# A routed feed-forward kernel: starting-up products ahead of the styles, a shorter list for the first expert, and its tokens turned and multiplied group by group

## The chip, the cores and the metric

The kernel runs on one core of one Trainium2 chip. The metric is the device time of one execution in microseconds (us). Five engines work side by side and are joined by semaphores: TensorE (PE; its weight loads are listed apart as PEld), VectorE (DVE), ScalarE (ACT), GpSimd (POOL) and SyncE (SP). SP and POOL also issue DMA transfers.

## What is computed

With B = 8 samples of L = 512 rows and C = D = 512 channels (N = 4096 rows), E = 8 experts of width 2048, and K = 1024 rows per expert:

```
styles = cond @ (affine_w / 16).T + affine_b          # 8 x 512
dcoefs = rsqrt(sum((weight * styles)**2) + 1e-8)      # 8 x 512
y      = clip(((x * styles) @ weight.T) * dcoefs + bias, -256, 256)
scores = softmax(y @ Wr)                              # 4096 x 8
G, idx = top_k(scores.T, 1024)                        # each expert takes its 1024 best rows
h      = gelu(y[idx] @ W1 + b1)                       # per expert, 1024 x 2048
out    = x + scatter_add(idx, G * (h @ W2 + b2))
```

Everything is float32. `idx` is a data-dependent list, so an expert's rows are fetched from memory with indirect DMAs, and they can't be fetched before the list is known.

## The kernel before

**Stage 1, the projection (0 to about 139 us).** The styles are the first work on TensorE: two products of `cond_sb` with `aff_sb` (lines 389 to 392; a float32 product is two instructions, so four), then one DVE operation (`style_rows`, line 395) and a turn back to columns (`turn_style`, line 403). Sample 0 is turned with TensorE (`turn_x0`, line 375), scaled and multiplied; samples 1 to 7 follow in `unit` (line 569). `in_order` (line 366) chains TensorE instructions so that they are issued in the order written; where it isn't used, the framework puts an engine's instructions into an order of its own, subject to data dependences. For each sample `score_softmax` (line 515) makes the eight scores of each row (`S`), the first expert's score (`S0`), copies of it (`reps`) and, against 64 thresholds, a table `ge` that is summed into `topc`.

**Stage 2, the first expert's list (139 to 162 us).** `route_first` (line 205) adds up the eight `topc` tables on TensorE (`tot_top`), picks the leading six bits of the threshold, finds the other 24 bits in six rounds of four (line 220: one DVE count, one TensorE product, three small DVE steps), marks the rows and ranks them; `lo` and `hi` are the rank's low seven bits and the rest. Meanwhile TensorE turns five late samples and SP stores them in `y_dram` (lines 698 to 708). `indices` (line 810) makes one-hot tables of `lo` (`oh`, 128 wide, in four parts for expert 0) and `hi` (`hot`, 8 wide), and multiplies them for the 32 groups of 128 rows (line 835, 32 products), which gives the 8 x 128 row numbers `idx`.

**Stage 3, the first expert's tokens (162 to about 182 us).** `fetch(0)` (line 1098) issues eight indirect DMAs on POOL (`gather`, line 865), groups 0 to 3 (the first half, i = 0) and then 4 to 7 (i = 1), each of 128 rows; after them POOL issues the copy of x to the output (line 1112). `prepare(0)` (line 890) turns each group with four TensorE instructions (line 910), copies the result to `xT` with two DVE copies (line 912), and at the end makes four sums of the halves (`left_sums`, line 881), each over 128 x 1024 elements, on DVE.

**Stage 4, the experts (from then to the end).** For each expert two passes of `hidden_unit` (line 956; four units `u`, each with 128 hidden columns of either half of the pass) and `out_unit` (line 1011). Both use a scheme of seven block products in place of eight: p1 = "11", p2 = "12", p6 = "s2", p7 = "s3", p5 = "s1", p3 = "s4", p4 = "22", where s1 to s4 are the sums. A product is four TensorE instructions of 128x512 in a hidden unit and eight of 128x256 in an output unit, all issued in `product` (line 950), so they stand under line 953 in the profile (`ps_a_h`, `ps_b_h`, `ps_c_h` for the hidden units). `in_turns` (line 924) runs the units, each one's last two products behind the first ones of the next; `between` puts other work behind a unit, such as `route_others` (line 713), which finds the other seven experts' lists on DVE behind unit 0 of the first pass. Buffers: the PSUM banks `a` and `c` exist twice, `b` once, `ps_t` (for turning) twice; the SBUF tag `xg` twice (the gathered tokens, and before them the one-hot table).

Of the kernel before, what the change touches and what calls it, by code (L numbers as in the profile page):

```python
# [25 lines left out]
def tile_modulated_expert_choice_ffn(  # L26
# [26 lines left out]
    GH = HALF // P  # L53
    GAIN = 1.0 / math.sqrt(W)
# [18 lines left out]

    ident = const.tile([P, P], F32, name="ident")
# [3 lines left out]
    ones = const.tile([P, P], BF16, name="ones")  # L78
    nc.gpsimd.memset(ones, 1.0)
# [22 lines left out]
    iota_hi = const.tile([P, KG], BF16, name="iota_hi")  # L102
    nc.gpsimd.iota(iota_hi, pattern=[[1, KG]], base=0, channel_multiplier=0,
# [15 lines left out]
    NR = (30 - TOP) // RB  # L119
    M = 1 << RB  # L120
# [84 lines left out]
    def route_first(p1c, reps, topc):  # L205
# [6 lines left out]
        for n in range(B):  # L212
            nc.tensor.matmul(tot, ones, topc[:, n, :], start=(n == 0), stop=(n == B - 1))
# [6 lines left out]
        for n in range(NR):  # L220
# [24 lines left out]
        nc.tensor.matmul(ps[:, 0, :, :].rearrange("p a t -> p (a t)"), ones, flat,  # L245
                         start=True, stop=True)
        nc.tensor.matmul(ps[:, 1, :, :].rearrange("p a t -> p (a t)"), upper, flat,
                         start=True, stop=True)
# [23 lines left out]
        nc.vector.tensor_scalar(part, pos_i, P - 1, None, op0=ALU.bitwise_and)  # L272
# [3 lines left out]
        nc.vector.tensor_scalar(part2, pos_i, 7, None, op0=ALU.logical_shift_right)  # L276
# [13 lines left out]
    with tc.tile_pool(name="p1c", bufs=1) as p1c, tc.tile_pool(name="p1", bufs=2) as p1, \  # L290
# [72 lines left out]

        behind = {}

        def in_order(make, engine="PE"):

            if engine in behind:
                with tc.issue_after(behind[engine].ins):
                    behind[engine] = make()  # L370
            else:
                behind[engine] = make()
            return behind[engine]
# [141 lines left out]
        def score_softmax(b, ps):  # L515

            lgT = p1s.tile([P, P], F32, tag="lgT", name=f"lgT_{b}", bufs=2)
            nc.scalar.copy(lgT, ps)
            lg4 = ps_small.tile([P, LT, SL], F32, tag="small", name=f"lg_{b}")
            in_order(partial(nc.tensor.transpose, lg4.rearrange("p t e -> p (t e)"), lgT, ident))  # L520
            lg = lg4[:, :, 0:E]
            mx = p1s.tile([P, LT], F32, tag="mx", name=f"mx_{b}")
            nc.vector.tensor_reduce(mx, lg, AX.X, ALU.max)
            ex = p1s.tile([P, LT, E], F32, tag="ex", name=f"ex_{b}")
            nc.vector.tensor_tensor(ex, lg, mx.unsqueeze(2).to_broadcast([P, LT, E]), ALU.subtract)
            nc.scalar.activation(ex, ex, AF.Exp)
            sm = p1s.tile([P, LT], F32, tag="sm", name=f"sm_{b}")
            nc.vector.tensor_reduce(sm, ex, AX.X, ALU.add)
            nc.vector.reciprocal(sm, sm)
            here = slice(b * LT, (b + 1) * LT)  # L530
            nc.vector.tensor_tensor(S[:, here, :], ex,
                                    sm.unsqueeze(2).to_broadcast([P, LT, E]), ALU.mult)
            nc.vector.tensor_copy(S0[:, here], S[:, here, 0])
            nc.vector.tensor_copy(reps[:, :, :, b],
                                  S0[:, here].unsqueeze(2).to_broadcast([P, ST_G, M]))
            ge = p1s.tile([P, 1 << TOP, LT], BF16, tag="getop", name=f"getop_{b}", bufs=2)
            nc.vector.tensor_tensor(ge, S0[:, here].unsqueeze(1).to_broadcast([P, 1 << TOP, LT]),
                                    top.bitcast(F32).unsqueeze(2).to_broadcast([P, 1 << TOP, LT]),
                                    ALU.is_ge)
            with nc.allow_low_precision("whole numbers up to 4"):  # L540
                nc.vector.tensor_reduce(topc[:, b, :], ge, AX.X, ALU.add)
# [150 lines left out]
        score_softmax(B - 1, lg)  # L692
# [3 lines left out]
        places = {0: route_first(p1c, reps, topc)}  # L696
# [113 lines left out]
    def indices(e):  # L810
# [7 lines left out]
            iota_hi.unsqueeze(1).to_broadcast([P, NT, KG]), ALU.is_equal,  # L818
# [6 lines left out]

        parts = 1 if e else 4
        for n in range(parts):
            here = slice(n * NT // parts, (n + 1) * NT // parts)
            nc.vector.tensor_tensor(  # L829
                oh[:, here, :], lo[:, here].unsqueeze(2).to_broadcast([P, NT // parts, P]),  # L830
                iota_lo.unsqueeze(1).to_broadcast([P, NT // parts, P]), ALU.is_equal,
            )
# [7 lines left out]
        nc.vector.tensor_copy(idx[:, e, :], idx_f)  # L840

# [10 lines left out]
    def gather(e, i):  # L852

        z = gp.tile([P, GH * YW], F32, tag="xg", name=f"xg_{e}_{i}")
        if e:
            rows = dram.tile([HALF, YW], F32, name=f"rows_{e}_{i}")
            z = z[:, 0 : GH * D].rearrange("p (t c) -> p t c", c=P)
        else:  # L860
            z = z.rearrange("p (g w) -> p g w", w=YW)
        for j in range(GH):
            g = i * GH + j
            to = gp.tile([P, YW], F32, tag="row", name=f"row_{e}_{g}", bufs=4) if e else z[:, j, :]
            sent = nc.gpsimd.indirect_dma_start(
                out=to[:, :], out_offset=None, in_=y_dram[:, :],
                in_offset=bass.IndirectOffsetOnAxis(ap=idx[:, e, g : g + 1], axis=0),
            )
            if e:
                nc.sync.dma_start(rows[j * P : (j + 1) * P, :], to)  # L870
        if e:
            for q in range(4):
                nc.sync.dma_start(z[q * TB : (q + 1) * TB, :, :],
                                  rows[:, q * P : (q + 1) * P].rearrange("(t a) c -> a t c", a=TB))
            with nc.allow_non_contiguous_dma(reason="512 values"):
                nc.sync.dma_start(gains[e][:, i * GH : (i + 1) * GH],
                                  rows[:, D + e : D + e + 1].rearrange("(g p) o -> p (g o)", p=P))
        gathered[e, i] = z
        return sent
# [9 lines left out]

    def prepare(e):  # L890

        xT = {}
        for i in range(2):
            for k in range(2):
                xT[i, k] = fx.tile([P, 2, HALF], F32, tag=f"xT{i}{k}", name=f"xT{i}{k}_{e}")
        gain = gains.pop(e)
        ngain = fx.tile([P, KG], F32, tag="ngain", name=f"ngain_{e}")
        for i in range(2):
            xg = gathered.pop((e, i))
            for k in range(2):  # L900
                if e:
                    nc.vector.transpose(
                        xT[i, k].rearrange("p j (t b) -> p t j b", b=TB),
                        xg[:, :, 2 * k * TB : 2 * (k + 1) * TB].rearrange("p t (j a) -> p t j a", a=TB))
            for j in range(0 if e else GH):
                g = i * GH + j
                nc.scalar.copy(gain[:, g : g + 1], xg[:, j, D + e : D + e + 1])
                ps = ps_t.tile([P, DC, P], F32, tag="t", name=f"ps_xg{e}_{g}")
                for dc in range(DC):
                    nc.tensor.transpose(ps[:, dc, :], xg[:, j, dc * P : (dc + 1) * P], ident)  # L910
                for k in range(2):
                    nc.vector.tensor_copy(xT[i, k][:, :, j * P : (j + 1) * P],
                                          ps[:, 2 * k : 2 * k + 2, :])
        nc.vector.tensor_scalar_mul(ngain, gain, -1.0)
        s = {n: fx.tile([P, 2, HALF], F32, tag=f"x{n}", name=f"x{n}_{e}")
             for n in ("s1", "s2", "s3", "s4")}
        left_sums(xT[0, 0], xT[0, 1], xT[1, 0], xT[1, 1], s)
        s["11"], s["12"], s["22"] = xT[0, 0], xT[0, 1], xT[1, 1]
        tokens[e] = s, gain, ngain
# [35 lines left out]

    def hidden_unit(e, p, u, H):

        s, _, _ = tokens[e]
# [6 lines left out]
        def mm(ps, left, right, start):  # L965
            product(ps, [blk[right][:, k, u * P : (u + 1) * P] for k in range(2)],
                    [s[left][:, k, :] for k in range(2)], start)

# [5 lines left out]
        def p1():  # L974
            st["a"] = bank("a", name, 2)
            mm(st["a"], "11", (0, 0), True)
            st["s1"] = snap(1)

        def p2():
            st["b"] = bank("b", name, 1)  # L980
            mm(st["b"], "12", (1, 0), True)
# [27 lines left out]
        return [p1, p2, p6, p7, p5, p3, p4]  # L1009
# [88 lines left out]
    def fetch(e):  # L1098
# [3 lines left out]
        for i in range(2):  # L1102
            sent = gather(e, i)
        return sent
# [5 lines left out]

    with tc.issue_after(fetch(0).ins):
        nc.gpsimd.dma_start(out.rearrange("b l d -> b (l d)").rearrange("b (r w) -> (b r) w", r=16),
                            x.rearrange("b l d -> b (l d)").rearrange("b (r w) -> (b r) w", r=16))
    prepare(0)
    for e in range(E):
        b2_sb = fx.tile([P, D], F32, tag="b2", name=f"b2_{e}")
        nc.sync.dma_start(b2_sb, b2[e, :].partition_broadcast(P))
        for p in range(NP):
            nxt = (e, p + 1) if p + 1 < NP else (e + 1, 0)
            H = fx.tile([P, U, 2, KG * P], F32, tag="H", name=f"H_{e}_{p}")  # L1120
# [5 lines left out]
            in_turns([partial(hidden_unit, e, p, u, H) for u in range(U)], work)  # L1126
# [48 lines left out]
```

## Time and profile before

| what | value |
|---|---|
| time, median of 3 runs | 1750.04 us (1749.76 to 1750.58) |
| the profiled execution's own time | 1749.67 us |
| its span, first to last instruction | 1747.9 us |
| PE busy in the span | 1708.3 us (98%) |
| DVE / ACT / POOL busy | 835.7 / 478.3 / 292.2 us |
| PE busy from 0 to 30 us | 23.86 of 30 us |
| PE busy from 152 to 172 us | 6.15 of 20 us |
| PE busy from 262 us to the end | 1474.83 of 1485.9 us |

The profiled execution took 1.8 us more than its span and 0.37 us less than the median. "Busy" counts an instruction from its start to its modelled end; TensorE instructions overlap, so what one of a row costs is read from the distance between starts. "PEclk" is the share of the full TensorE clock that was granted. The release of a wait is inferred; "issue" means that nothing the profile shows was waited for.

### The profile page before, as it was taken

The numbers are of one execution on the slowest core, as the hardware profiler recorded it, in microseconds if no ns is written. First come the engines' busy times: TensorE is split into PE (matmuls) and PEld (weight loads), VectorE is DVE, ScalarE is ACT, GpSimd is POOL, SyncE is SP. The second block draws the span as 40 slices with busy tenths as digits, with TensorE's granted clock in tenths as the row PEclk, the third lists the DMA queues.
The fourth block names the chain that finished last, engine by engine and source line by source line (L and its number), as shares of the span: only waits on it lengthen the run. The fifth ranks groups of instructions, "written<-read, shape, count | busy, mean of one in ns | idle before, by whom it ended". The sixth has DMA issues, their size and how long they took to land.

```text
span 1747.9 us, 17152 instructions
## 1 busy us (share of the span) xinstructions
PE 1708.3 (98%) x6522; PEld 1128.9 (65%) x6522; DVE 835.7 (48%) x1465; ACT 478.3 (27%) x842; POOL 292.2 (17%) x238
## 2 busy tenths in 40 slices
PE   8995999999999999999999999999999999999997
PEld 4774475665748485666748485766758484756656
DVE  5885883624536254524535254614445254614341
ACT  3543312223131322223231313222231313222231
POOL 0112013020222013020312013110312012110202
PEclk9997999999999999999999999999999999999999
DMA  9625627541573227441574237442574137332403
GB/s 205 172 50 177 211 49 165 121 90 48 96 201 67 54 52 173 109 84 50 98 197 79 48 64 179 89 80 55 108 184 88 45 66 182 79 79 61 84 0 49
DMA packets 143250, 178.57 MB, mean 102 GB/s; under 512 B 16824, under 2 KB 92856, under 8 KB 143040
## 3 DMA queue, kind: packets, MB, share of 16 engines
q1 hardware_dynamic: 118240, 115.19, 24.5%
q0 software_dynamic: 24912, 62.27, 21.1%
q8 instruction: 51, 0.84, 0.2%
q14 instruction: 31, 0.25, 0.1%
q10 hardware_dynamic: 16, 0.02, 0.0%
HBM read 120.46 MB, written 65.37 MB: 106 GB/s over the span
## 4 chain that ended last, share of the span: by engine, by line
PE 87%; DVE 2%; issue 0%; DMA 0%; POOLq 0%; POOL 0%; DVEq 0%
PE ps_a_o L953 25%; PE ps_a_h L953 25%; PE ps_c_o L953 12%; PE ps_c_h L953 12%; PE ps_b_h L953 6%; PE ps_b_o L953 6%; DVE mark L736 0%; PE ps_idx L835 0%; DVE oh L829 0%; DMA xg<-y_dram,idx 0%; PE ps_xg L910 0%; DVE ps_b_h L982 0%; POOLq L1171 0%; DVE hs_o L884 0%; DVE hs_o L883 0%
## 5 line engine op out<-in xcount | busy, mean ns | idle before, releaser
L1065 POOL DMA_INDIRECT out<-o_o,idx x128 | 212.3, 1659 | 1248.8 <-DVE o_o L1062 553.2
L953 PE MATMUL ps_a_o<-w_t,hs_o 128*128 128x256 f32 x1024 | 243.6, 380 | 1.2
L953 PE MATMUL ps_a_h<-xs,w_t 128*128 128x512 f32 x512 | 241.1, 593 | 0.0
L953 PEld LDWEIGHTS ps_a_o<-w_t,hs_o 128*128 128x128 f32 x1024 | 192.3, 190 | 33.4 <-issue 7.0
L971 ACT COPY snap_h<-ps_a_h 128x512 f32<-128x512 f32 x192 | 111.7, 582 | 236.9 <-PE ps_a_h L953 231.8
L953 PEld LDWEIGHTS ps_a_h<-xs,w_t 128*128 128x128 f32 x512 | 97.0, 190 | 123.0 <-issue 122.1
L1032 ACT ACTIVATE snap_o<-ps_a_o,gain 128x256 f32<-128x256 f32 x128 | 60.6, 474 | 347.5 <-PE ps_a_o L953 347.5
L997 DVE TENSOR_TENSOR snap_h<-snap_h,ps_c_h 128x512 f32<-128x512 f32 x64 | 43.9, 686 | 217.5 <-ACT snap_h L971 217.5
L982 DVE TENSOR_TENSOR ps_b_h<-ps_b_h,snap_h 128x512 f32<-128x512 f32 x64 | 44.7, 699 | 202.9 <-PE ps_b_h L953 202.9
L953 PE MATMUL ps_a_h<-xT,w 128*128 128x512 f32 x256 | 125.6, 598 | 0.0
L953 PE MATMUL ps_a_o<-w,H 128*128 128x256 f32 x512 | 124.1, 379 | 0.0
L953 PE MATMUL ps_c_o<-w,hs_o 128*128 128x256 f32 x512 | 123.8, 379 | 0.0
L953 PE MATMUL ps_a_h<-xs,w 128*128 128x512 f32 x256 | 122.0, 599 | 0.0
L953 PE MATMUL ps_a_o<-w,hs_o 128*128 128x256 f32 x512 | 121.5, 380 | 0.0
L953 PE MATMUL ps_b_o<-w,H 128*128 128x256 f32 x512 | 121.2, 379 | 0.0
L953 PE MATMUL ps_b_h<-xT,w 128*128 128x512 f32 x256 | 120.8, 593 | 0.0
L953 PE MATMUL ps_c_h<-xs,w 128*128 128x512 f32 x256 | 120.5, 593 | 0.0
L953 PE MATMUL ps_c_h<-xT,w_t 128*128 128x512 f32 x256 | 120.5, 593 | 0.0
L953 PE MATMUL ps_c_o<-w_t,H 128*128 128x256 f32 x504 | 119.1, 379 | 0.0
L953 PEld LDWEIGHTS ps_a_o<-w,H 128*128 128x128 f32 x512 | 97.1, 190 | 27.0 <-issue 15.5
L953 PEld LDWEIGHTS ps_a_o<-w,hs_o 128*128 128x128 f32 x512 | 96.0, 190 | 21.4 <-ACT snap_o L1032 8.9
L953 PEld LDWEIGHTS ps_c_o<-w,hs_o 128*128 128x128 f32 x512 | 97.1, 190 | 14.0 <-issue 0.6
(248 smaller groups left out, 1935.9 us busy)
## 6 DMA issues: line engine op xcount, KB each, us to landing
w<-in_w SPq DMA_DIRECT2D x120, 512.0 KB, 4.0
rows<-row SPq DMA_DIRECT2D x56, 260.0 KB, 4.0
xg<-rows SPq DMA_DIRECT2D x56, 256.0 KB, 6.6
x<-in_x SPq DMA_DIRECT2D x28, 256.0 KB, 8.8
y_dram<-ytok SPq DMA_DIRECT2D x5, 1024.0 KB, 4.4
w<-in_w SPq DMA_DIRECT2D x32, 128.0 KB, 4.1
y_dram<-ytok POOLq DMA_DIRECT2D x12, 256.0 KB, 4.8
b<-in_b SPq DMA_DIRECT2D x8, 256.0 KB, 4.0
```

Of the source, the lines that this page charges most:

```text
L953: nc.tensor.matmul(ps, lefts[k], rights[k], start=(start and k == 0), stop=(k == n - 1), skip_group_check=True)
L971: nc.scalar.copy(t, st["a"])
L982: added = nc.vector.tensor_add(st["b"], st["b"], st["s1"])
L997: nc.vector.tensor_add(st["u4"], st["u4"], st["c"])
L1032: nc.scalar.mul(t, st["a"], scale)
L1065: nc.gpsimd.indirect_dma_start(out=last_rows[g] if e == E - 1 else out_rows, out_offset=bass.IndirectOffsetOnAxis(ap=idx[:, e, g : g + 1], ...
```

## The change

- A helper `idle` issues products of a constant table of ones with itself (128x512 in bf16) into an unused bank; nine are issued ahead of the first product of the styles. The table `ones` is filled ahead of the other constants. `in_order` and its chain now serve the whole kernel.
- In `score_softmax`, `S0` is made straight from the exponentials and their sums. For the last sample `S` is made after `ge`, and `ge` isn't summed on DVE: `route_first` adds its four columns per threshold with four products.
- The first expert's rank is split into six low bits (`LO` = 64) and the rest (`HI` = 16): `first_indices` takes the place of `indices(0)`. The one-hot table of the low digits is half as wide, that of the high ones twice, one of the two products of the latter goes to ACT, and each of the 32 groups takes two TensorE products of 64 weight columns each, into partitions 0 to 63 and 64 to 127. Each part's products are issued behind the part.
- `first_tokens` takes the place of `gather(0, i)` and `prepare(0)`: groups are fetched in the order 0, 4, 1, 5, 2, 6, 3, 7. For each pair both groups are turned, the first half is copied by DVE and the second by ACT, the four sums are made for these 128 columns, and p1 and p2 of hidden units 0 and 1 are made for these 128 columns (`begin`). The gains are copied in two instructions at the end.
- `gather` and `prepare` lose their branches for expert 0.

```diff
+    IDLE0 = 9
+    def idle(n, ps):
+
+        for _ in range(n):
+            in_order(partial(nc.tensor.matmul, ps.rearrange("p (a k) -> p a k", k=P), ones,
+                             ones.unsqueeze(1).to_broadcast([P, HALF // P, P]), start=True, stop=True))
+
+    ones = const.tile([P, P], BF16, name="ones")
+    nc.gpsimd.memset(ones, 1.0)
+    idle(IDLE0, ps_mm.tile([P, HALF], F32, tag="c", name="ps_idle0", bufs=2))
...
+    LO, HI = P // 2, 2 * KG
...
-        for n in range(B):
-            nc.tensor.matmul(tot, ones, topc[:, n, :], start=(n == 0), stop=(n == B - 1))
+        for n in range(B - 1):
+            nc.tensor.matmul(tot, ones, topc[:, n, :], start=(n == 0), stop=False)
+        for t in range(LT):
+            nc.tensor.matmul(tot, ones, last_top[:, :, t], start=False, stop=(t == LT - 1))
...
-            nc.vector.tensor_copy(S0[:, here], S[:, here, 0])
+            last = b == B - 1
+            if not last:
+                scores()
+            nc.vector.tensor_mul(S0[:, here], ex[:, :, 0], sm)
...
+            if last:
+                with tc.issue_after(done.ins):
+                    scores()
+                return ge
...
+    def first_indices():
+
+
+        lo, hi = places[0]
+        hot = gp.tile([P, 2 * GH * YW], BF16, tag="xg", name="hot_0")[:, 0 : NT * HI].rearrange(
+            "p (t h) -> p t h", h=HI)
+        nc.vector.tensor_tensor(hot, hi.unsqueeze(2).to_broadcast([P, NT, HI]),
+                                iota_hi.unsqueeze(1).to_broadcast([P, NT, HI]), ALU.is_equal)
...
+        nc.scalar.mul(val[:, :, 0, :], hot, iota_p[:, 0:1])
+        nc.vector.tensor_tensor(val[:, :, 1, :], hot,
+                                iota_t.unsqueeze(2).to_broadcast([P, NT, HI]), ALU.mult)
+        parts = 4
+        ps = ps_small.tile([P, 2, KG], F32, tag="small", name="ps_idx0")
+        for n in range(parts):
+            here = slice(n * NT // parts, (n + 1) * NT // parts)
+            nc.vector.tensor_tensor(
+                oh[:, here, :], lo[:, here].unsqueeze(2).to_broadcast([P, NT // parts, LO]),
+                iota_lo[:, 0:LO].unsqueeze(1).to_broadcast([P, NT // parts, LO]), ALU.is_equal)
+            for t in range(NT)[here]:
+                for q in range(P // LO):
+                    in_order(partial(
+                        nc.tensor.matmul, ps[q * LO : (q + 1) * LO, :, :], oh[:, t, :],
+                        val[:, t, :, :].rearrange("p a (g q) -> p q a g", q=P // LO)[:, q, :, :],
+                        start=(t == 0), stop=(t == NT - 1), skip_group_check=True))
...
+    def first_tokens(started):
+
+
+        half = [gp.tile([P, GH * YW], F32, tag="xg", name=f"xg_0_{i}").rearrange(
+            "p (g w) -> p g w", w=YW) for i in range(2)]
+        for j in range(GH):
+            for i in range(2):
+                g = i * GH + j
+                sent = nc.gpsimd.indirect_dma_start(
+                    out=half[i][:, j, :], out_offset=None, in_=y_dram[:, :],
+                    in_offset=bass.IndirectOffsetOnAxis(ap=idx[:, 0, g : g + 1], axis=0))
...
+        xT, s, gain, ngain = token_tiles(0)
+        for j in range(GH):
+            cols = slice(j * P, (j + 1) * P)
+            for i in range(2):
+                ps = ps_t.tile([P, DC, P], F32, tag="t", name=f"ps_xg_{i}_{j}")
+                for dc in range(DC):
+                    in_order(partial(nc.tensor.transpose, ps[:, dc, :],
+                                     half[i][:, j, dc * P : (dc + 1) * P], ident))
+                for k in range(2):
+                    if i:
+                        copied = nc.scalar.copy(xT[i, k][:, :, cols], ps[:, 2 * k : 2 * k + 2, :])
+                    else:
+                        nc.vector.tensor_copy(xT[i, k][:, :, cols], ps[:, 2 * k : 2 * k + 2, :])
+            left_sums(*[xT[i, k][:, :, cols] for i in range(2) for k in range(2)],
+                      {n: t[:, :, cols] for n, t in s.items()})
+            for f in started:
+                f(cols)
...
+        def begin(cols):
+            s = tokens[e][0]
+
+            for to, left, right in (("a", "11", (0, 0)), ("b", "12", (1, 0))):
+                if to not in st:
+                    st[to] = bank("c" if u and to == "b" else to, f"{name}_{to}", 1 if to == "b" and not u else 2)
+                for k in range(2):
+                    in_order(partial(nc.tensor.matmul, st[to][:, cols],
+                                     blk[right][:, k, u * P : (u + 1) * P], s[left][:, k, cols],
+                                     start=(cols.start == k == 0), stop=(k == 1),
+                                     skip_group_check=True))
...
-    with tc.issue_after(fetch(0).ins):
-        nc.gpsimd.dma_start(out.rearrange("b l d -> b (l d)").rearrange("b (r w) -> (b r) w", r=16),
-                            x.rearrange("b l d -> b (l d)").rearrange("b (r w) -> (b r) w", r=16))
-    prepare(0)
+    first_indices()
+    gains[0] = fx.tile([P, KG], F32, tag="gain", name="gain_0", bufs=2)
+    H = fx.tile([P, U, 2, KG * P], F32, tag="H", name="H_0_0")
+    early = [hidden_unit(0, 0, u, H, early=True) for u in range(2)]
+    first_tokens([begin for begin, _ in early])
```

## The prediction

> **What bounds the kernel now.** I read the page's 40 slices first, then the busy time and clock by stretches, then the instructions in order of time in three places that the change touches. From 262 us on TensorE is busy for 1474.83 of 1485.9 us, and nothing of that part is changed; so I ask only how much earlier TensorE gets there. Two places are loose: the first 30 us and 152 to 172 us.
>
> ```profile
> PE   8995999999999999999999999999999999999997
> ...
> 148.00:152.00 4.00, 2.17 (x14) 1.47 (x14) 2.85 (x13) 1.79 (x4) 0.00 (x0) 1.00 1.01 376
> 152.00:156.00 4.00, 0.22 (x2) 0.10 (x1) 3.28 (x19) 0.00 (x0) 0.00 (x0) 0.76 0.50 190
> 156.00:160.00 4.00, 0.77 (x17) 0.59 (x17) 4.00 (x6) 0.00 (x0) 0.00 (x0) 0.50 0.21 70
> 172.00:176.00 4.00, 3.85 (x16) 2.55 (x16) 2.21 (x7) 0.76 (x4) 1.56 (x2) 0.68 1.28 437
> 176.00:178.00 2.00, 2.00 (x9) 1.15 (x8) 1.76 (x7) 1.38 (x3) 0.00 (x0) 1.00 0.82 328
> ```
>
> In the stretches the columns are PE, PEld, DVE, ACT, POOL, then the granted clock, the DMA share and GB/s. The fourth slice (131 to 175 us) is the 5; in it the clock falls to half at about 154 and is back in about 174.7.
>
> ```profile
> 4.98 1.87 PE L372 MATMUL ps_style<-aff_sb,cond_sb 128*8 128x512 f32 x2 [4.98 <-DMA cond_sb<-in_condT]
> 6.64 1.91 PE L370 MATMUL ps_style<-aff_sb,cond_sb 128*8 128x512 f32 x2
> 8.48 1.98 PE L370 MATMUL ps_x<-ident,x 128*128 128x128 f32 x8
> 8.59 1.08 DVE L395 SCALAR_TENSOR_TENSOR style_rows<-ps_style,affb_in 8x512 f32<-8x512 f32 x1 [2.98 <-PE ps_style L370]
> 10.40 0.64 PE L370 MATMUL ps_styleT<-ident,style_rows 8*128 8x8 f32 x4
> 12.75 3.60 PE L370 MATMUL ps_y<-xmT,wa_sb 128*128 128x512 f32 x8
> ```
>
> The clock column says 1.00 here, but the distances say otherwise: four style instructions take 3.5 us (0.87 each), the same size at 12.75 takes 0.45. TensorE starts slow and is fast from some point after 10.4.
>
> ```profile
> 138.59 0.42 DVE L537 TENSOR_TENSOR getop<-S,top 128x256 bf16<-128x256 f32 x1
> 139.04 0.42 DVE L541 TENSOR_REDUCE topc<-getop 128x64 bf16<-128x256 bf16 x1
> 139.81 0.23 DVE L216 SCALAR_TENSOR_TENSOR ok_top<-tot_top,top 128x64 f32<-128x64 f32 x1 [0.35 <-PE tot_top L213]
> ...
> 156.45 4.62 DVE L829 TENSOR_TENSOR oh<-lo,iota_lo 128x1024 bf16<-128x1024 bf16 x4
> 161.13 0.38 PE L835 MATMUL ps_idx<-val,oh 128*128 128x16 bf16 x8 [0.75 <-DVE oh L829]
> 163.16 1.04 POOL L865 DMA_INDIRECT xg<-y_dram,idx  x1 [23.88 <-issue]
> ...
> 166.65 1.12 PE L910 MATMUL ps_xg<-ident,xg 128*128 128x128 f32 x4 [5.14 <-DMA xg<-y_dram,idx]
> 173.03 1.80 PE L953 MATMUL ps_a_h<-xT,w 128*128 128x512 f32 x2
> 176.84 1.88 PE L953 MATMUL ps_b_h<-xT,w 128*128 128x512 f32 x4
> ```
>
> From 133 to 162 a chain of small DVE steps ends last; from 162 to 176 the eight fetches, which POOL issues about 1.27 us apart; from 176.7 on TensorE.
>
> [...]work from 4.98 is slow past 10.4, work from 168.1 is slow until 174.7[...]. [...]No row of before has 64 bf16 columns. [...]the trace has 0.42 us for 256 elements and 1.22 for 1024[...], also for these bf16 tables.
>
> **1. Nine products ahead of the styles.** `ones` is filled in 0.2 us from 0.75, so they can start at about 1.05. A bf16 one of 512 columns should take half a slow float32 instruction of 0.87 (estimate 0.43), nine 3.85 us: they end at 4.9, where `aff_sb` lands (4.95), so they delay the styles by nothing, at worst by one product. [...]the clock rises between about 4.2 and 7.6. Averaged, the four style instructions end at 7.2 instead of 8.42. The DVE row step follows 0.17 later and takes 1.08, so the styles can be turned at 8.55. Before they waited until 10.39, because the eight slow turns of x ended then; fast turns of 0.11 end at about 8.1. That is 1.84, and the turn of the styles itself falls from 0.64 to about 0.41: **2.0 us** (1.1 to 2.5). The weights `wa_sb` land 6.2 to 6.7 after issues at 2.8 to 4.2, at 9.0 to 10.9, so products at 10.7 find them, and x_1 lands by about 21 and is wanted at 22.9. From 30 to 130 TensorE is busy for 97.3 us, waits for DMAs nowhere, so the gain is handed on whole.
>
> **2. The last sample's scores.** S0 comes one DVE step earlier (138.05 instead of 138.27: 0.22). The sum of `ge` (139.04 to 139.46) goes; four products take the place of one (some 0.03 apart by the six at 129.99: 0.1), and may queue behind the four turns of `reps` (0.66). Of 0.6 I count **0.35** (0.1 to 0.6). Making S after `ge` lies in DVE's wait for TensorE, and its store has 20 us. The seven earlier samples change a copy for a product: nothing.
>
> **3. The list.** DVE: `hot` and the second product grow from 256 to 512 elements, +0.27 each; the first product goes to ACT, -0.20 (155.91 to 156.11); the first part of `oh` has 512 elements, not 1024, -0.53. So TensorE starts at 157.5 instead of 157.72. ACT is idle there; its product takes about 0.6 and is done by 157.0. The parts then come 0.60 apart[...]. TensorE has 16 pairs a part: the 128 columns of before came 27 ns apart (0.38 for eight, less a last one of 0.19) at the half clock. [...]TensorE is the bound, and its 64 pairs end at 161.0 instead of 161.5: **0.5 us**. At 27 ns DVE would be the bound and the gain 1.6; at 67 (load and product in turn) it is -0.4. The bank and number of fetches are as before, and so is the 1.23 us from `idx` to the first.
>
> **4. The tokens.** Fetches are as many and as far apart; I use the old landing times, 166.5 to 175.7. A pair takes eight turns and 16 pieces of 128 columns (2 units x 2 products x 2 k x 2 instructions). Slow, at 0.213 each, that is 5.1 us; fast, with 0.114 for a turn (the late samples: eight in 0.91) and 0.107 for a piece (a quarter of 0.43; two weight loads in 0.30 show that loads can follow at 0.11), 2.6, plus about 0.3 for the first DVE copy (0.2 + 0.38 after the turns of the first half, with the second's turns beside them). Pairs land 2.5 apart, so TensorE, not the fetch, is now the bound: pair 0 from 166.65 to 172.4, clock up at about 173 (171.5 to 174.9), pairs 1 to 3 end at 175.6, 178.5 and 181.3. DVE has 0.76 + four sums of 256 elements (1.5) a pair, 2.3, which lies beside it; the last sums are there at 181.6. ACT's two copies (0.85) and later the table load (1.28) have cover too: p6 and p7 take 3.4 us of TensorE before p5 wants ACT's second copy. By 181.6 the new kernel has 16 instructions of line 953 done. Before it had 14 at 181.35 (2+2+4+2+4), so 14.6, and had made the turn of S (0.22). So 1.4 x 0.43 - 0.22: **0.4 us** (-0.2 for a late clock, 1.1 for an early one).
>
> The sum is 2.0 + 0.35 + 0.5 + 0.4 = 3.25 us. Against 1749.67 of the profiled execution that gives **1746.4 us**. That execution is 0.37 under the median of 1750.04; I leave that[...]. Where the moved start of `route_others` falls changes nothing that I can price: TensorE waited only 1.1 us for it.
>
> **Rivals.**
> - *The list and the tokens give more*: 64 columns load in 27 ns (+1.1), and TensorE is woken by the idle-free run of 64 pairs[...] (+0.7 to 1.1). 1749.67 - 5.2 = 1744.4. For it: weight loads of 32 float32 columns stand 25 ns apart. Against it: the five idle us of the fetch lie between.
> - *The start is not handed on*: [...]the styles wait behind the ninth product; part 1 gives 0.7 and the tokens nothing: 1748.3.[...] Against it: no wait for a DMA stands behind the styles.
> - *Slower: pieces bound by weight loads.* If the load of a piece can't lie beside the piece before, as long as itself, each costs 0.107 + 0.19 (the mean load) = 0.30. 64 x 0.19 = 12 us more: 1758.6. It turns the sign from 0.16 a piece on. Against it: turns have as short a product and come 0.114 apart, with a load each.
>
> **Chances.** Forecast 0.53, more 0.24, start not handed on 0.17, slower 0.06. About 0.2% (3.5 us, 1746.54) can be told from no change. The forecast lies on that line and half of it counts as faster, 0.29, half as the same, 0.24; "more" is faster, "not handed on" the same, the last slower. Faster 0.53, same 0.41, slower 0.06. The range takes in "more" to its far end and "not handed on": 1743.6 to 1748.9; what is left out is the slow rival and the far tails.
>
> **What would show it.** Nine products from about 1 to 4.9, and ps_styleT near 8.6 instead of 10.40; the first fetch at about 160.3 (163.16 less 2.85); products of `ps_idx` 53 ns apart, ending after DVE; pieces 0.11 apart; TensorE without gaps from about 165 to 178, shifted. It is wrong if the styles are turned at 10, if the pieces come 0.2 or more apart, or if TensorE waits for sums after the last pair by more than 1 us.

## The result and the profile after

The changed kernel takes **1746.51 us** (median of 17 runs, 1744.58 to 1748.62) where the one before, beside it, takes 1749.87 (1748.92 to 1753.08, 17 runs): ratio 0.9981, 95% interval [0.9974, 0.9988]. The 17 runs lie in two groups: eight from 1744.58 to 1746.08 (middle 1745.69), eight from 1747.08 to 1748.62 (middle 1747.69), one between. The profiled execution is of the later group: 1747.71 us, span 1745.9. It is 1.96 under the profiled one of before (1749.67).

The page's slices first, TensorE's share and its clock, in tenths:

```profile
PE   9996999999999999999999999999999999999997
...
PEclk9998999999999999999999999999999999999999
```

Where before had an 8 in the first slice and a 5 in the fourth there is now a 9 and a 6. The stretches (PE, PEld, DVE, ACT, POOL, granted clock, DMA share, GB/s) put the difference at the list:

```profile
148.00:152.00 4.00, 2.06 (x16) 1.43 (x14) 2.73 (x14) 2.18 (x4) 0.00 (x0) 1.00 0.99 360
152.00:156.00 4.00, 0.22 (x2) 0.10 (x1) 3.03 (x16) 0.00 (x0) 0.00 (x0) 0.76 0.58 214
156.00:160.00 4.00, 2.35 (x64) 2.05 (x64) 3.30 (x7) 0.72 (x1) 0.00 (x0) 0.50 0.29 70
...
172.00:176.00 4.00, 3.84 (x32) 3.51 (x32) 3.19 (x10) 1.29 (x4) 0.10 (x1) 1.00 1.09 391
176.00:178.00 2.00, 2.00 (x20) 1.86 (x18) 1.36 (x4) 0.00 (x0) 0.00 (x0) 1.00 1.05 426
```

The start, in order of time (start, duration, engine, line, operation, count, and in brackets the idle time ahead and who ended it):

```profile
1.41 3.13 PE L81 MATMUL ps_idle<-ones 128*128 128x512 bf16 x8
...
5.05 1.88 PE L81 MATMUL ps_style<-aff_sb,cond_sb 128*8 128x512 f32 x4 [0.51 <-DMA cond_sb<-in_condT]
...
6.96 1.05 DVE L405 SCALAR_TENSOR_TENSOR style_rows<-ps_style,affb_in 8x512 f32<-8x512 f32 x1 [1.36 <-PE ps_style L81]
7.96 0.99 PE L81 MATMUL ps_x<-ident,x 128*128 128x128 f32 x6 [0.60 <-DMA x<-in_x]
8.88 0.64 PE L81 MATMUL ps_styleT<-ident,style_rows 8*128 8x8 f32 x4
...
10.68 1.10 PE L81 MATMUL ps_x<-ident,x 128*128 128x128 f32 x4 [1.16 <-DVE xmT L81]
11.58 4.88 PE L81 MATMUL ps_y<-xmT,wa_sb 128*128 128x512 f32 x8
16.30 0.63 PE L81 MATMUL ps_x<-ident,x 128*128 128x128 f32 x4
```

The styles are turned at 8.88, not 10.40: 1.52 gained. But the eight products of `ps_y` that follow take 4.88 us where before they took 3.60, and the next turns of x stand at 16.30 against 16.19 before. Against this profile of before, the start gained nothing.

The scores, the list and the first tokens:

```profile
138.33 0.42 DVE L553 TENSOR_TENSOR getop<-S,top 128x256 bf16<-128x256 f32 x1
...
139.43 0.22 DVE L238 SCALAR_TENSOR_TENSOR ok_top<-tot_top,top 128x64 f32<-128x64 f32 x1 [0.58 <-PE tot_top L235]
...
154.96 0.17 DVE L299 CAST hi<-part 128x32 bf16<-128x32 int32 x1
155.51 0.69 DVE L864 TENSOR_TENSOR hot<-hi,iota_hi 128x512 bf16<-128x512 bf16 x1 [0.38 <-DMA y_dram<-ytok]
...
157.33 1.89 DVE L876 TENSOR_TENSOR oh<-lo,iota_lo 128x512 bf16<-128x512 bf16 x3
157.51 2.35 PE L81 MATMUL ps_idx<-oh 128*64 128x16 bf16 x64 [4.85 <-DVE oh L870]
159.91 0.17 DVE L886 TENSOR_REDUCE idx_f<-ps_idx 128x8 f32<-128x16 f32 x1 [0.70 <-PE ps_idx L81]
...
161.62 1.04 POOL L961 DMA_INDIRECT xg<-y_dram,idx  x1 [21.72 <-issue]
...
165.06 1.11 PE L81 MATMUL ps_xg<-ident,xg 128*128 128x128 f32 x4 [5.19 <-DMA xg<-y_dram,idx]
...
172.18 0.71 PE L81 MATMUL ps_a_h_a<-xT,w 128*128 128x128 f32 x4
...
174.06 1.04 PE L81 MATMUL ps_xg<-ident,xg 128*128 128x128 f32 x8
...
180.07 1.88 PE L1023 MATMUL ps_a_h_a<-xs,w_t 128*128 128x512 f32 x4
```

In before, the two moments that are not shown above are these:

```profile
16.19 0.63 PE L370 MATMUL ps_x<-ident,x 128*128 128x128 f32 x4
...
155.24 0.17 DVE L278 CAST hi<-part 128x32 bf16<-128x32 int32 x1
```

Step by step (before's moment less after's), the turns of x behind the first `ps_y` give 16.19 - 16.30 = -0.11, the cast of `hi` 155.24 - 154.96 = 0.28, the first fetch 163.16 - 161.62 = 1.54, and the end 1.96. So the parts of this execution are: start -0.1, scores 0.4, list 1.3, and tokens 0.4, which is what is left of the 1.96.

### The profile page after: what moved, and what is told of

Its sections match the earlier page's. It is cut to its first block, busy times and chain, and to the rows that moved or that the text cites. A ratio compares the mean times of both kernels' runs of the same rounds, so it can differ in the third digit from the quotient of the medians.

```text
span 1745.9 us, 17351 instructions
## 1 busy us (share of the span) xinstructions
PE 1712.4 (98%) x6614; PEld 1136.2 (65%) x6614; DVE 830.6 (48%) x1467; ACT 479.5 (27%) x845; POOL 291.9 (17%) x238
## 4 chain that ended last, share of the span: by engine, by line
PE 93%; DVE 4%; ACT 1%; DMA 1%; issue 1%; POOL 0%; POOLq 0%; SPq 0%; DVEq 0%; ACTq 0%
PE ps_a_o L1023 25%; PE ps_a_h L1023 23%; PE ps_c_o L1023 12%; PE ps_c_h L1023 12%; PE ps_b_o L1023 6%; PE ps_b_h L1023 6%; PE ps_ya L81 2%; DVE oh L845 1%; PE ps_yc L81 1%; PE ps_y L81 1%; ACT xmT L496 1%; DVE mark L756 1%; PE ps_yt L723 1%; PE ps_a_h_a L1023 0%; PE ps_yb L81 0%
## 5 line engine op out<-in xcount | busy, mean ns | idle before, releaser
L1023 PE MATMUL ps_a_h<-xs,w_t 128*128 128x512 f32 x496 | 233.4, 592 | 0.0
L1054 ACT COPY snap_h<-ps_a_h 128x512 f32<-128x512 f32 x186 | 108.0, 581 | 230.1 <-PE ps_a_h L1023 227.1
L1023 PE MATMUL ps_a_h<-xT,w 128*128 128x512 f32 x248 | 120.7, 594 | 0.0
L1023 PE MATMUL ps_a_h<-xs,w 128*128 128x512 f32 x248 | 118.2, 599 | 0.0
L1023 PE MATMUL ps_b_h<-xT,w 128*128 128x512 f32 x248 | 116.8, 593 | 0.0
```

The costliest lines, as they stand in the source:

```text
L1023: nc.tensor.matmul(ps, lefts[k], rights[k], start=(start and k == 0), stop=(k == n - 1), skip_group_check=True)
L1054: nc.scalar.copy(t, st["a"])
```

## The experiments

"Before" is the kernel before on the same chip; ratios are to it, with 95% intervals in brackets.

### Which part gives what: each alone

Two take up the start: the nine products put into the kernel before, and the changed kernel without them. Of each edit only the main line is shown; the helpers that it needs come with it.

```diff
--- before.py
+++ e1
+    idle(IDLE0, ps_mm.tile([P, HALF], F32, tag="c", name="ps_idle0", bufs=2))
--- after.py
+++ e2
-    idle(IDLE0, ps_mm.tile([P, HALF], F32, tag="c", name="ps_idle0", bufs=2))
```

> The kernel before with the nine products of ones ahead of the styles and nothing else of the change. Theory (from the profile after): the early clock is lost again when TensorE waits for the turned styles[...], so single runs spread by some 3 us and the median is about 1.0 us below before. Rival (the sum on record): 2.0 us, handed on whole, with little spread. A second rival: nothing at all (0.0), as in the one profiled execution of the changed kernel.

> The changed kernel without the nine products. Theory: 2.2 to 2.5 us below before, and its runs lie as close together as those of before (under 2 us), where the changed kernel's spread over 4. Rival (the sum on record): 1.25 us below before, as the start is worth 2.0 of 3.25.

Two put one other part into the kernel before: the 64 by 16 list (`first_indices`), and the paired order of the tokens with the early pieces (`first_tokens`, `begin`).

```diff
--- before.py
+++ e3
-        indices(e)
+        indices(e) if e else first_indices()
--- before.py
+++ e4
-    ... gather(0, i) ... prepare(0)
+    ... first_tokens(started) ...
```

> The kernel before with the 64 x 16 list alone. Theory: 64 weight columns load in about 27 ns at the half clock, DVE is the bound, and the list ends 1.6 us earlier; some of it is lost to the wait of the hot table for the last store of y, 0.1 to 0.3: 1.4 us below before. Rival (the sum on record): 53 ns a pair, TensorE is the bound, 0.5 us.

> The kernel before with the paired order of fetches, the sums by 128 columns and the early products, on the old list. Theory and the sum on record agree: 0.4 us below before, -0.2 to 1.1[...]. Rival: the early products are worth the 12 instructions that they bring forward, 5 us less the 3 us by which TensorE gets free later: 2 us.

| kernel | median us (range, runs) | before | ratio |
|---|---|---|---|
| e1, start alone | 1748.40 (1747.08 to 1750.49, 21) | 1749.82 | 0.9992 [0.9986, 0.9999] |
| e2, all but the start | 1748.04 (1745.96 to 1749.01, 21) | 1749.82 | 0.9986 [0.9979, 0.9993] |
| e3, list alone | 1748.22 (1747.10 to 1749.56, 13) | 1749.82 | 0.9990 [0.9982, 0.9999] |
| e4, tokens alone | 1749.25 (1748.08 to 1750.76, 13) | 1749.82 | 0.9995 [0.9987, 1.0003] |

The start is worth 1.4 us alone, and 1748.04 - 1746.51 = 1.5 within the whole. The list is worth 1.6; by its profile, from the cast of `hi` at 155.08 to the first fetch at 161.67, 6.59 us against 7.92 before, 1.3. The tokens' 0.6 can't be told from nothing by time alone. The intervals overlap, so the order of start and list is not shown. That both count rests on intervals that just leave out 1, and that the list gives more than 0.5 on its profile:

```profile
155.08 0.17 DVE L297 CAST hi<-part 128x32 bf16<-128x32 int32 x1
...
161.67 1.04 POOL L905 DMA_INDIRECT xg<-y_dram,idx  x1 [22.55 <-issue]
```

Two expectations were missed: e1 gave 1.4 where 1.0 was expected, and e2 1.8 where 2.2 to 2.5 was; its runs spread over 3.05 us, not under 2. Why is in the next part.

### Why the start comes through only sometimes

The granted clock of the changed kernel's profile rises at 3.92, falls to half at 10.74 and is back at 14.16. The half clock lasts 3.41 us; TensorE's busy time in as long a stretch ahead of it:

```profile
7.33:10.74 3.41, 1.65 (x12) 1.44 (x11) 1.83 (x5) 0.62 (x1) 0.00 (x0) 1.00 1.03 301
```

Half of it is waiting, for x (0.60) and for DVE's first scaled block (1.16) above all; the other half is turns alone, without a product. The rise shows in the eight `ps_idle` too: 3.13 us for them, in place of 3.62 at half clock throughout. If the waits are the cause, products that fill them keep the clock: four behind those of the styles, five behind their turn.

```diff
--- after.py
+++ e5
-    idle(IDLE0, ps_mm.tile([P, HALF], F32, tag="c", name="ps_idle0", bufs=2))
+    ps_idle = ps_mm.tile([P, HALF], F32, tag="c", name="ps_idle0", bufs=2)
+    idle(IDLE0, ps_idle)
...
+        idle(4, ps_idle)
         style_rows = p1c.tile([B, 2, C]
...
         dcoef = p1c.tile([P, CC, B], F32, name="dcoef")
+        idle(5, pss[3])
```

> The changed kernel with four more products of ones behind the styles' own and five more behind their turn, so that TensorE stays busy until the first projection products. Theory: the clock no longer falls there, the start's 2.0 us come whole in every run instead of 1.5 on average: 0.6 to 1.0 us below the changed kernel (4.0 to 4.4 below before), runs closer together. Rival (the fall of the clock costs nothing, or the nine products had given all): no difference from the changed kernel, and its profile shows products of the first projection 0.43 us apart without any gain at the end.

It takes 1746.04 us (1744.83 to 1746.95, 15 runs; before 1749.73; 0.9978 [0.9970, 0.9985]). The stretch of its profile that answers to the line above is full, the clock stays up, and the products of `ps_y` take 3.60 again:

```profile
7.40:10.80 3.40, 3.40 (x21) 2.27 (x19) 1.94 (x4) 0.62 (x1) 0.00 (x0) 1.00 0.99 300
```

None of its 15 runs lies above 1746.95; of the changed kernel's 17, eight do. So the later group is gone. The median is only 0.5 lower, where 0.6 to 1.0 was expected, and the intervals overlap. A part of the reason is that the added products stand in the way themselves: the styles are turned at 9.13, not 8.88, and the next turns of x stand at 14.93, where the profiles that kept their clock without added products have 14.06 to 14.77.

The other experiments' profiles, whose start is that of the changed kernel, then show both cases. One of the earlier kind is e9's (below):

```profile
1.41 3.62 PE L81 MATMUL ps_idle<-ones 128*128 128x512 bf16 x8
...
8.53 0.64 PE L81 MATMUL ps_styleT<-ident,style_rows 8*128 8x8 f32 x4
10.33 0.72 PE L81 MATMUL ps_x<-ident,x 128*128 128x128 f32 x4 [1.16 <-DVE xmT L81]
10.88 3.60 PE L81 MATMUL ps_y<-xmT,wa_sb 128*128 128x512 f32 x8
```

Here all nine products ran slow (eight in 3.62), the four of the styles behind them, from 4.96 on, fast (1.88), and the clock stayed: it is 1.00 in every stretch from 4.90 to 15.13. Of the seven profiles with this start alone (after, e1, e6, e7, e9, e11, e12), three (after, e1, e11) have `ps_y` at 4.8 to 5.2 us and four at 3.60. In e7's the turns of x behind them come early:

```profile
14.06 0.63 PE L81 MATMUL ps_x<-ident,x 128*128 128x128 f32 x4
```

That is 16.19 - 14.06 = 2.1 us gained, against -0.1 in the profile of after, and about the distance of the two groups of runs. In between lies e12, whose clock rose later still (its style products take 2.73): 14.77, 1.4 gained. The mean clock of each run fits, as 3.4 us at half clock are 0.001 of the span: it is 0.993 in all eight runs of the later group and 0.994 in seven of the nine others. **The earliest clock was the worst**: in the three profiles in which it fell, the last of the nine products already ran fast (from 3.54 on three in 1.00 us in after and 0.90 in e1, from 3.81 on two in 0.59 in e11); in the four in which it stayed they ran slow to the end (three in 1.49). Why an early rise is lost and a later one is not, the profiles don't show.

The nine products are not what makes the clock fall, though. e2 and e4, which lack them, run their eight turns of x fast (1.23 us from 8.32 and 8.19 on, where before took 1.98), and have the clock down at 11.53 and 11.37, and e2's runs show the same two clocks (0.994 in the ten fastest, 0.993 in the eleven others). So the turns of x come late there too:

```profile
17.05 0.63 PE L81 MATMUL ps_x<-ident,x 128*128 128x128 f32 x4
```

The -0.1 compares with a profile of before that kept its clock. Over the profiles without further products at the styles, these turns start at 16.03 (e3), 16.19 (before), 16.89 (e4) and 17.05 us (e2) without the nine products, and at 14.06 to 16.30 with them; the means, 16.54 and 15.06, are 1.5 us apart, which is what e1 and e2 measured.

### The list's new wait

In the profile after, `hot` (line 864) starts 0.55 after the cast of `hi`, 0.38 of it put down to a store of `ytok`: its table borrows the buffer of the fetched rows, `xg`, and the late stores, as the wait says, still read that memory. One experiment gives the table of high digits a buffer of its own; another swaps the two pools `fx` and `gp`, so that `xg` lies elsewhere.

```diff
--- after.py
+++ e6
-        hot = gp.tile([P, 2 * GH * YW], BF16, tag="xg", name="hot_0")[:, 0 : NT * HI].rearrange(
+        hot = rt0.tile([P, NT * HI], BF16, name="hot_0").rearrange(
--- after.py
+++ e9
-    fx = ctx.enter_context(tc.tile_pool(name="fx", bufs=1))
     gp = ctx.enter_context(tc.tile_pool(name="gp", bufs=2))
+    fx = ctx.enter_context(tc.tile_pool(name="fx", bufs=1))
```

> The changed kernel with the one-hot table of the high digits in memory that no late row of y shares. Theory: the 0.38 us for which DVE waits for the last store of y goes, and DVE's list starts that much earlier; 0.3 us below the changed kernel, and the profile shows the table 0.1 to 0.2 us behind the cast of the high digits instead of 0.55. Rival: the wait moves to the next table, which still lies there, and nothing is gained.

> The changed kernel with the pool of the gathered rows placed ahead of the pool of the turned ones, so that none of the list's tables shares memory with a late row of y. Theory: DVE's list starts 0.36 to 0.42 us earlier and stands on DVE alone; 0.4 us below the changed kernel, no wait of the list for a store of y in its profile. Rival: the tables then wait for something else that lay there (the turns of the late samples on TensorE), or the first fetch waits for the stores instead; nothing gained.

e6: 1745.35 us (1743.73 to 1746.77, 10 runs; before 1749.73; 0.9975 [0.9966, 0.9985]). Its profile has the wait no more:

```profile
152.75 0.17 DVE L299 CAST hi<-part 128x32 bf16<-128x32 int32 x1
152.96 0.69 DVE L864 TENSOR_TENSOR hot<-hi,iota_hi 128x512 bf16<-128x512 bf16 x1
```

0.21 from cast to table in place of 0.55: 0.34 us, shown; from the cast to the first fetch it is 6.40 us in place of 6.66. The 1.2 us by which its median is lower are more than that and within the overlap of the intervals; its profile stands at 152.75 because its start came through. e9: 1746.20 us (1745.47 to 1747.65, 9 runs; before 1750.48; 0.9977 [0.9967, 0.9986]), and `hot` still waits 0.38 for the store. Which buffer the store holds after the swap is open.

The rival of e6, that the wait moves to the next table, came in e8 (below), which has e6's edit among others:

```profile
154.30 0.69 DVE L868 TENSOR_TENSOR hot<-hi,iota_hi 128x512 bf16<-128x512 bf16 x1
...
155.84 0.69 DVE L874 TENSOR_TENSOR oh<-hot,iota_t 128x512 bf16<-128x512 bf16 x1 [0.85 <-DMA y_dram<-ytok]
```

The other tables still lie in `xg`, so the edit takes the wait away only where the store is done by then.

### A clock kept up into the tokens

In the profile after, the list's products and the whole first pair of tokens run at half clock; it is back at 171.2. Products of ones could bridge this: 14 behind the ranks, 16 behind those of the list.

```diff
--- after.py
+++ e7
+        idle(14, ps_mm.tile([P, HALF], F32, tag="c", name="ps_idle1", bufs=2))
         tot = p1c.tile([P, 2, NT + 1], F32, name="rtot0")
...
+        idle(16, ps_mm.tile([P, HALF], F32, tag="c", name="ps_idle2", bufs=2))
         idx_f = rt2.tile([P, KG], F32, tag="idx_f", name="idx_f_0")
```

> The changed kernel with 14 products of ones behind the ranks and 16 behind the list's products, so that TensorE is busy until the first rows land. Theory: the turns and the first pieces run at the full clock, TensorE keeps up with the fetches, and the last piece ends 1.3 to 2.1 us earlier; 1.3 to 1.8 us below the changed kernel. Rival: the fetches or DVE's sums were the bound all along; under 0.4 us.

**1743.40 us** (1742.95 to 1746.11, 6 runs; before 1749.73; 0.9968 [0.9956, 0.9980]), the lowest median of all kernels here (as a ratio to before, e12 below is as low). The clock is 1.00 from 150 to 176:

```profile
157.07 0.42 PE L81 MATMUL ps_idx<-oh 128*64 128x16 bf16 x16 [0.18 <-DVE oh L877]
157.43 3.63 PE L81 MATMUL ps_idle<-ones 128*128 128x512 bf16 x16
...
159.24 1.04 POOL L963 DMA_INDIRECT xg<-y_dram,idx  x1 [21.57 <-issue]
...
162.75 0.66 PE L81 MATMUL ps_xg<-ident,xg 128*128 128x128 f32 x4 [1.70 <-DMA xg<-y_dram,idx]
...
175.56 1.88 PE L1025 MATMUL ps_a_h_a<-xs,w_t 128*128 128x512 f32 x4
```

From the first fetch to the end of the pieces are 16.3 us (159.24 to 175.56), in the profile after 18.45 (161.62 to 180.07): 2.1 us for the clock in the first pair. The other 1.0 of the difference in medians is within the two kernels' spread.

Which of the two groups counts? One kernel has only the 16 behind the list.

```diff
--- after.py
+++ e12
+        idle(16, ps_mm.tile([P, HALF], F32, tag="c", name="ps_idle2", bufs=2))
         idx_f = rt2.tile([P, KG], F32, tag="idx_f", name="idx_f_0")
```

> The changed kernel with only the second group of added products: 16 behind the list's own, none behind the ranks. Those of the list still run at half clock (154 to 157), so the 16 take about 6.8 us at half speed and would reach past the first fetch's landing at 165, up to 164.5[...]. Theory (what counts is that TensorE is at full clock when the first pair is turned): the clock rises between 161 and 164.5, the tokens gain 1.5 to 2.2 us, 1744.6 (1744.0 to 1745.5). Rival (only an unbroken clock from the ranks on is worth anything): no gain, 1746.5.

1743.98 us (1743.29 to 1744.49, 5 runs; before 1750.16; 0.9965 [0.9952, 0.9979]).

```profile
158.32 6.33 PE L81 MATMUL ps_idle<-ones 128*128 128x512 bf16 x16
...
160.12 1.04 POOL L962 DMA_INDIRECT xg<-y_dram,idx  x1 [21.74 <-issue]
...
164.49 1.25 PE L81 MATMUL ps_xg<-ident,xg 128*128 128x128 f32 x8
...
176.52 1.90 PE L1024 MATMUL ps_a_h_a<-xs,w_t 128*128 128x512 f32 x4
```

The list ran at half clock, the 16 slowly (6.33), and yet from fetch to the end of the pieces are 16.4 us. So it is the clock at the first pair that counts, and not an unbroken one: the rival of that expectation falls. That the list's products run slow costs little, since DVE's tables pace them: from the cast of `hi` to the first fetch it is 6.63 us here and 6.52 in e7.

### Do they add up?

Three kernels put the edits together: e8 those of e5, e6 and e7; e10 those of e5, e7 and e9; e11 those of e6 and e7.

> The three edits together. If they add: 2.3 to 3.1 us below the changed kernel, 5.7 to 6.5 below before. If the full clock only moves the wait to the fetches: what the products at the start and the table give, 0.9 to 1.3 below the changed kernel.

> The pools swapped, the four and five products of ones at the styles, and 14 and 16 behind the ranks and the list. If the three gains add (0.5 + 0.4 + 2.2): 3.1 us below the changed kernel, 6.5 below before, with no fall of the clock from 4 us to the end in its profile. Rival, from the run with all three edits that lay above the one with the list's products alone: the products at the styles take back what they give when the clock rises late, and the sum stays at 5.3 to 6 below before.

> The changed kernel with both groups of added products of the list (14 behind the ranks, 16 behind the list's own) and the table of high digits in a buffer of its own, without added products at the styles. If the two edits add, as they touch different waits (0.4 us of DVE behind the late stores, 2.2 us of TensorE at half clock), it should stand at 1743.0 (1742.4 to 1743.6), a little below the run with the added products alone (1743.4). If the added products need the store's wait to be short by chance, and what spoilt the run of all three edits was the table or the wait behind it, it stands near 1744.4 again; if it was the products at the styles, 1743.

| kernel | median us (range, runs) | before | ratio |
|---|---|---|---|
| e8 | 1744.39 (1744.23 to 1746.02, 7) | 1749.73 | 0.9970 [0.9959, 0.9981] |
| e10 | 1750.17 (1744.95 to 1751.92, 21) | 1750.48 | 0.9995 [0.9988, 1.0001] |
| e11 | 1744.89 (1743.60 to 1745.73, 6) | 1750.16 | 0.9969 [0.9957, 0.9981] |

They don't add. In e8's profile, that of its slowest run, the wait for the store has moved to the next table, cast to fetch takes 7.16 us, and the clock falls at 157.08 in spite of the added products: TensorE had nothing to do from the last of the 14, at 154.82, to 157.24 (2.42 us). e11 was expected at 1743.0. Its profile is one where the clock fell at the start (`ps_y` 4.78, cast of `hi` at 154.81, in e7's at 152.72); from the cast to the first fetch it takes 6.22 us (e7 6.52), from there to the end of the pieces 16.33. So both edits did their part in this execution, and the chance at the start hides them; with five to seven runs each, e7, e8, e11 and e12 can't be put in an order.

e10 fell flat for another reason, which its profile shows:

```profile
155.72 0.69 DVE L868 TENSOR_TENSOR hot<-hi,iota_hi 128x512 bf16<-128x512 bf16 x1 [1.57 <-DMA y_dram<-ytok]
...
169.09 1.04 PE L81 MATMUL ps_xg<-ident,xg 128*128 128x128 f32 x8
...
173.00 0.76 DVE L986 COPY xT<-ps_xg 128x256 f32<-128x256 f32 x2 [3.54 <-remote]
...
173.48 0.84 PE L81 MATMUL ps_a_h_a<-xT,w 128*128 128x128 f32 x4 [3.35 <-DVE xT L986]
```

The wait for the store is 1.57 here. Then the second pair's turns end by 170.13, but the copies that wait for them start at 173.00; TensorE idles 3.35 us, and the clock, which had fallen at 156.85 and come back at 163.68, falls once more at 173.92. From the first fetch to the end of the pieces are 21.3 us, 5 more than in e7. Four of its 21 runs are at 1744.95 to 1746.02, one at 1747.99, and 16 at 1749.90 or more, about 5 above the four: most seem to have it, but only one was profiled. The profile of e4, its second slowest run, shows the same at the same place, shorter:

```profile
172.54 1.04 PE L81 MATMUL ps_xg<-ident,xg 128*128 128x128 f32 x8
...
174.92 0.76 DVE L947 COPY xT<-ps_xg 128x256 f32<-128x256 f32 x2 [2.79 <-PE ps_xg L81]
```

The changed kernel's profile has nothing of it: its copies start 0.64 to 0.76 us behind the start of the turns, where e4's start 2.38 and e10's 3.91 behind. What holds them is open. In both cases the release comes shortly after POOL's last issue (171.68 + 0.60 in e10, 173.75 + 0.60 in e4). This was not tried by itself.

## Why the prediction was right, and where its steps were not

1746.4 was forecast and 1746.51 measured. That the total came so close is luck: two terms were off in opposite senses.

- **1. The start: 2.0 forecast, 1.4 to 1.5 measured.** The step that failed is "the gain is handed on whole". It looked for waits for DMAs after 30 us and never asked whether the clock, once up, stays up through the waits between 7.3 and 10.7. Its range for the rise, 4.2 to 7.6, was an estimate, and its early end was too late as well: in the profile after the clock rose at 3.92. Nor did it price the landing of x: the turns of x were to end at 8.1, but the last six wait for it till 7.96, so the styles are turned at 8.88 and not near 8.55; and their turn takes 0.64 at either clock, not 0.41. Against the profile of before, the gain is 2.1 where the clock holds, as forecast, and -0.1 where it falls; the two groups of runs are equally large. The rival "the start is not handed on" is thus what about half of the executions do, for a reason that it did not name: a clock that rises early and falls again. It fell although TensorE was busy for 1.65 of the 3.41 us ahead (48%), with turns alone.
- **2. The scores: 0.35 forecast, 0.4 in the profile** (139.81 to 139.43 for `ok_top`; 0.39 from the turns of x to the cast of `hi`). Not tried alone.
- **3. The list: 0.5 forecast, 1.3 by the profile, 1.6 by e3.** The step that failed is "TensorE is the bound": the forecast took the two products of a group one after the other, and they run side by side. In the trace the two, into partitions 0 to 63 and 64 to 127, start 0 to 7 ns apart in the last three parts, and the next two most often 53 ns later, at half clock. So 53 ns is the price of two pairs, not of one, some 27 ns each. The last 16 end at 159.86, 0.64 after the last part of `oh` (157.33 + 1.89 = 159.22). DVE is the bound, and the 1.6 that the forecast named for this case came, less a wait for a store (0.34) that it did not see: the change moved the tables into a buffer that a store still read. The forecast's 53 ns a pair was its author's estimate, as before has no load of 64 bf16 columns; at full clock the distance from two pairs to the next two is 32 ns (e7, where sixteen take 0.42 us).
- **4. The tokens: 0.4 forecast, 0.4 left by the profile, 0.6 in e4, where no gain at all lies in the interval too.** Pieces are 0.12 apart (172.18 to 174.06 for 16), a pair takes 3.0 us, TensorE waits for no sum; the clock came at 171.2, a little ahead of the early end of its range. In e7 the same code is 2.1 us faster: the half clock in the first pair, which the forecast took as given, was the largest thing that the experiments found left.
- **The rivals.** "The list and tokens give more" was right that the list gives more, but a single load in 27 ns is not what made it so: the 27 ns come from two loads side by side, 53 ns for both. It was wrong in the tokens. "Slower", with pieces 0.30 apart, did not come.

The range: its far end at 1743.6 is about where the changed kernel with a kept clock stands (e7 1743.40), its near end at 1748.9 just past the latest run (1748.62).

## What to carry to other kernels

Products that only warm the clock brought its rise forward here (to 3.92 us in after, from 10.75 in before), and by the two groups of runs it fell again in about half of the executions (at 10.74 in after): look at what TensorE does in the microseconds behind the rise, and fill those waits too (e5, where the later group of runs is gone), or the gain can be given back. Put such products where the array would otherwise idle just ahead of the work that counts (16 behind the list were worth 2.1 us in the first pair), not only at the earliest place. A table that borrows a buffer inherits the last reader of that buffer, a store included (0.34 us in after against e6).

## What the runs showed of the hardware

- The clock fell behind stretches of 3.41 us in which TensorE was busy for 1.65 (after), 2.07 (e1), 2.19 (e2) and 2.22 us (e4). It stayed through the first waits in e5, with 3.40 of 3.40 us busy, and at the list of e7, with only 1.54 us busy in the 3.41 from 152.02 on (nothing from 153.44 to 155.31). So the busy time alone doesn't tell whether it falls, and what does is not shown.
- By the distances between products 512 float32 columns took 0.43 us at full clock (3.60 us for eight `ps_y` in e5) and 0.87 ahead of the rise (3.50 us for the four of the styles in before); 512 bf16 columns took 0.22 (3.63 us for sixteen `ps_idle` in e7) and 0.43 (3.62 us for eight in e9).
- Two loads of 64 bf16 columns for the two halves of the output partitions ran side by side, each with a product of 16 columns: two every 53 ns at half clock (after) and two every 32 ns at full clock (e7). With 128 columns a load, before, it was one every 27 ns at half clock (0.38 us for eight).
- Copies that waited for nothing but a finished turn, as far as the profile shows, started up to 2.9 us behind its end (170.13 to 173.00 in e10); the cause is open.
